# The first image of a convolution and attention block: one set of filter sums in another buffer, another order of the first loads, and BatchNorm's factors on GpSimd

## The chip, the core and the metric

The kernel runs on one core of a Trainium2 chip. Such a core has TensorE (PE: matrix products), VectorE (DVE), ScalarE (ACT), GpSimd (POOL) and SyncE (SP, which here issues transfers), each with an instruction stream of its own; they wait for each other through semaphores. On-chip memory is SBUF; products land in PSUM. The metric is the device time of one execution in microseconds (us). The kernel before takes 2331.0 us, the median of three runs (2330.74 to 2331.12).

## The reference

The input is a batch of eight images of 512 channels and 32x32 positions. All is float32. `silu`, `softmax` and 3x3 convolutions are the usual ones; `bn` is BatchNorm with given mean and variance.

```python
# x: (8, 512, 32, 32); C = 256, N = 2 blocks, 4 heads of 64
def cbs(x, w, p, pad):
    return silu(bn_eval(conv2d(x, w, pad), p))

def bot_attention(x, qkv_w, rw, rh):
    qkv = conv2d(x, qkv_w, 0)                       # 1x1
    q, k, v = ...                                   # (8, 4, 64, 1024) each
    logits = einsum('bhdi,bhdj->bhij', q, k + rw + rh) * 64 ** -0.5
    return einsum('bhij,bhdj->bhdi', softmax(logits), v)

def block(x):
    t = cbs(x, cv1_w, cv1_bn, 0)                    # 1x1, 512 -> 512
    ys = [t[:, :C], t[:, C:]]                       # y0, y1
    for i in range(N):
        z = cbs(ys[-1], m_cv1_w[i], m_cv1_bn[i], 1)     # 3x3, 256 -> 256
        z = bot_attention(z, m_qkv_w[i], m_rw[i], m_rh[i])
        z = silu(bn_eval(conv2d(z, m_cv2_w[i], 0), m_cv2_bn[i]))
        ys.append(ys[-1] + z)
    return cbs(concatenate(ys, axis=1), cv2_w, cv2_bn, 0)

out = x + block(group_norm(x, 32 groups))
```

## The kernel before

The kernel goes through the images one after the other. TensorE's stages of an image are: `cv1` (a 1x1 convolution; in the program `ps`, line 386), the first 3x3 convolution (`c_ps`, line 970), the projections to q, k, v, the attention (`l_ps`, `av_ps`), `m2` (`m_ps`, line 994), the second 3x3 convolution, its attention, and the last 1x1 convolution. The `cv1` of the next image is done in pieces inside the attention of the image before it. VectorE, ScalarE and GpSimd prepare operands and read results.

**Filter sums.** The 3x3 convolutions work on sums of taps and sums of pixels, so that fewer products are needed. The sums of pixels, `v_in`, come from `tiles_in`; the sums of taps, `u`, come from the raw taps by `make_u`. There are three kinds (pairs 0, 1, 2), two halves of output channels (`oc`) and two halves of input channels (`k`). They are made once, during the first image, stored to DRAM and loaded for the later ones.

```python
def make_u(i, u, raw):
    rows, g1 = raw
    g0, g2 = rows[:, 0], rows[:, 1]
    ...
    if i == 2:
        nc.scalar.copy(u[:, :, 0:3:2], rows[:, :, 0::2])
        tt(minus, ...); tt(plus, ...); return tt(minus, ...)     # lines 331 to 333
    if i == 0:
        tt(b, g0, g2, ALU.add); tt(a, ...); tt(b, ...)           # lines 335 to 337
    else:
        stt(b, g2, 4.0, g0, ...); stt(a, ...); stt(b, ...)       # lines 339 to 341
    tt(minus, ...); tt(plus, ...); return stt(minus, ...)        # lines 343 to 345
```

**The ring.** Large weights and filter sums share five buffers under one name; a new tile waits until one of the five is read for the last time.

```python
def ring(shape, name):
    return const.tile(shape, F32, tag="u", name=name, bufs=5)

def new_u(name):
    return ring([P, NM, 2, NC, P], name)

def make(n, oc, pairs, ks=range(NM)):
    for k in ks:
        for i in pairs:
            if k == 0:
                us[oc, i] = new_u("u_new")
            last = make_u(i, us[oc, i][:, k], raws[n, oc, k])
            if k == NM - 1:
                nc.gpsimd.dma_start(u_dram[n][oc][i], us[oc, i])
    return last
```

**The first loads.** Transfers are issued in this order; a chunk of `x` is 512 KB, a piece of raw taps 576 KB, each half of `w1` 512 KB (two of its four row blocks).

```python
xs = [load_x(act, 0, c, NX) for c in range(NX // 2)]       # chunks 0 and 1
...
raws = {(0, 0, 0): load_raw(0, 0, 0, "k")}
load_w1_half(0)
xs += [load_x(act, 0, c, NX) for c in range(NX // 2, NX)]  # chunks 2 and 3
...
load_w1_half(1)
raws[0, 0, 1] = load_raw(0, 0, 1, "v")
... # BatchNorm's parameters, the other raws, the weights of the blocks
```

**The start.** GroupNorm is done in two parts, chunks 0 and 1, then 2 and 3. `tc.issue_after(x)` only tells the scheduler that what follows stands behind `x`.

```python
_, _, (_, read, _) = s.group_norm_part(xs[: NX // 2])
norm = s.group_norm_part(xs[NX // 2 :])
with tc.issue_after(read.ins):
    with tc.issue_after(loaded.ins):
        made = make_u(2, u_first[2][:, 0], raws[0, 0, 0])
    next(norm)
...
with tc.issue_after(made.ins):                              # BatchNorm's factors
    nc.vector.tensor_scalar(rstd, bnp[:, :, 3], BN_EPS, None, ALU.add)
    nc.gpsimd.tensor_tensor(rstd, rstd, mhalf[:, :NBN], ALU.pow)
    made = make_u(0, u_first[0][:, 1], raws[0, 0, 1])
with tc.issue_after(made.ins):
    nc.vector.tensor_tensor(sh, bnp[:, :, 0], rstd, ALU.mult)
    nc.vector.tensor_tensor(bh, bnp[:, :, 2], sh, ALU.mult)
    nc.vector.tensor_tensor(bh, bnp[:, :, 1], bh, ALU.subtract)
    for at in bn_m1:
        last = nc.vector.tensor_scalar(sh[:, at : at + NM], ..., -1 / 12, None, ALU.mult)
```

**From the first attention to the second convolution.** `behind` holds work that is put between pieces of the attention. In image 0 this is how the filter sums of block 1 come about: `u(1, 0, ..)` first, then of the second half pair 2 (which is only stored and loaded again later), pair 0, and after the attention pair 1.

```python
ao, check = s.attention_fast(0, z, b * N * NM * NH, behind, sq.get(0), t)
made = make(1, 1, [1]) if b == 0 else None
with tc.issue_after(made.ins) if made else nullcontext():
    last = s.m2(0, ao, y1, lambda oc, half: inner(y2, oc, half))    # adds at line 1002
if six: ...
elif more:
    s.cv1(w1, xs, nxt, y1n, Y0S)         # image 0: the last two pieces of the next cv1
vs = s.tiles_in(y2)
z, t = s.conv3x3(1, vs, u_of(1), True)
```

At the end of the attention `second()` loads the raw taps for pair 1 where k and v of the attention were: `raws[1, 1, k] = load_raw(1, 1, k, "kv"[k])`. The tile `q` is written by the projections, read by the logits and written again by the projections of the next block.

Of the kernel before, what the change touches and what calls it, by code (L numbers as in the profile page):

```python
# [44 lines left out]
F32 = mybir.dt.float32  # L45
I32 = mybir.dt.int32
AF = mybir.ActivationFunctionType
ALU = mybir.AluOpType
# [4 lines left out]
P = 128  # L53
BN_EPS = 1e-3
# [7 lines left out]
def kernel(  # L62
# [16 lines left out]
    nc = tc.nc  # L79
# [4 lines left out]
    NX = C1 // P  # L84
    NM = C // P
# [8 lines left out]
    NC = 4  # L94
# [3 lines left out]
    act = fast.enter_context(tc.tile_pool(name="act", bufs=1))  # L98


    def load_x(pool, b, c, bufs):
        xt = pool.tile([P, HW], F32, tag="x", name="x", bufs=bufs)
        src = x[b, ts(c, P), :] if isinstance(b, int) else x[bass.ds(b, 1), ts(c, P), :][0]
        nc.sync.dma_start(xt, src)
        return xt

    xs = [load_x(act, 0, c, NX) for c in range(NX // 2)]


    def ring(shape, name):  # L110
        return const.tile(shape, F32, tag="u", name=name, bufs=5)
# [8 lines left out]
    def load_w1_half(i):  # L120
        ks = slice(i * NX // 2, (i + 1) * NX // 2)
        nc.sync.dma_start(w1[:, ks], cv1_w.rearrange("(k p) o -> p k o", p=P)[:, ks])
# [9 lines left out]
    def rows_of_raw(raw):  # L132
        rows = raw.rearrange("p (r c) o -> p r c o", c=3)
        return rows[:, 0::2], rows[:, 1]

    def load_raw(n, oc, k, tag, bufs=1):
        raw = act.tile([P, 9, P], F32, tag=tag, name="raw", bufs=bufs)
        nc.sync.dma_start(raw, m_cv1_w[n, ts(k, P), :, ts(oc, P)])
        return rows_of_raw(raw)
# [11 lines left out]
        return rows_of_raw(raw[:, 0:9]), (both, mid)  # L151

    raws = {(0, 0, 0): load_raw(0, 0, 0, "k")}
    load_w1_half(0)
    xs += [load_x(act, 0, c, NX) for c in range(NX // 2, NX)]

# [40 lines left out]
    bnp = const.tile([P, NBN, 4], F32, name="bnp")  # L197
# [117 lines left out]
    def new_u(name):  # L315
        return ring([P, NM, 2, NC, P], name)
# [9 lines left out]
        stt, tt = nc.vector.scalar_tensor_tensor, nc.vector.tensor_tensor  # L326
        a, b = u[:, 0, 0:3], u[:, 1, 0:3]
        plus, minus = u[:, :, 1], u[:, :, 3]
        if i == 2:
            nc.scalar.copy(u[:, :, 0:3:2], rows[:, :, 0::2])  # L330
            tt(minus, rows[:, :, 0], rows[:, :, 2], ALU.add)
            tt(plus, minus, rows[:, :, 1], ALU.add)
            return tt(minus, minus, rows[:, :, 1], ALU.subtract)
        if i == 0:
            tt(b, g0, g2, ALU.add)
            tt(a, b, g1, ALU.add)
            tt(b, b, g1, ALU.subtract)
        else:
            stt(b, g2, 4.0, g0, ALU.mult, ALU.add)
            stt(a, g1, 2.0, b, ALU.mult, ALU.add)  # L340
            stt(b, g1, -2.0, b, ALU.mult, ALU.add)

        tt(minus, u[:, :, 0], u[:, :, 2], ALU.add)
        tt(plus, minus, plus, ALU.add)
        return stt(minus, minus, 2.0, plus, ALU.mult, ALU.subtract)

    def load_u(n, oc, i):
        u = new_u("u")
        nc.sync.dma_start(u, u_dram[n][oc][i])
        return u  # L350
# [10 lines left out]
    def inner(yp, c, half):  # L361
        return yp[:, c, 1 + half * ROWS : 1 + (half + 1) * ROWS, :].rearrange("p h w -> p (h w)")

    def stages(act, small, ps_big, ps_av, n_pt):
# [120 lines left out]
        def gn_stats(mv, c, xt):  # L485
            st = small.tile([P, NH, 6], F32, tag="st", name="st")
            for half in range(NH):
                nc.vector.bn_stats(st[:, half, :], xt[:, ts(half, HALF)])
            nc.vector.bn_aggr(mv[:, c, :], st.rearrange("p a b -> p (a b)"))
# [9 lines left out]
        def gn_mean(mv, n=NX, pool=ps_big, tag="big"):  # L499

            ps = pool.tile([P, n], F32, tag=tag, name="gm_ps")
            over_groups(ps, mv[:, :, 0])
            gm = small.tile([P, n], F32, tag="gm", name="gm")
            dev = small.tile([P, n], F32, tag="dev", name="dev")
            nc.vector.tensor_copy(gm, ps)
            nc.vector.tensor_tensor(dev, mv[:, :, 0], gm, ALU.subtract)
            nc.vector.tensor_tensor(dev, dev, dev, ALU.mult)
            averaged = nc.vector.tensor_tensor(dev, dev, mv[:, :, 1], ALU.add)
            return gm, dev, averaged
# [9 lines left out]
        def group_norm_part(xts):  # L519


            n = len(xts)
            mv = small.tile([P, n, 2], F32, tag="mv", name="mv", bufs=2)
            for c in range(n):
                gn_stats(mv, c, xts[c])
            yield
            gm, dev, averaged = gn_mean(mv, n, ps_av, "av")
            yield averaged
            gr, multiplied, read = gn_rstd(dev, n, ps_av, "av")
            shift = small.tile([P, n], F32, tag="dev", name="shift")  # L530
            nc.gpsimd.tensor_tensor(shift, gm, gr, ALU.mult)
            nc.gpsimd.tensor_scalar(shift, shift, -1.0, None, ALU.mult)
            for c in range(n):
                for half in range(NH):
                    part = xts[c][:, ts(half, HALF)]
                    applied = nc.scalar.activation(
                        part, part, AF.Identity, scale=gr[:, c : c + 1], bias=shift[:, c : c + 1]
                    )
            yield multiplied, read, applied

        def group_norm(xts):

# [708 lines left out]
    s = stages(act, small, ps_big, ps_av, 3)  # L1251
# [4 lines left out]
    Y0S, Y1S = range(NM), range(NM, 2 * NM)  # L1256
    us = {}

    def make(n, oc, pairs, ks=range(NM)):

        for k in ks:
            for i in pairs:
                if k == 0:
                    us[oc, i] = new_u("u_new")
                last = make_u(i, us[oc, i][:, k], raws[n, oc, k])
                if k == NM - 1:
                    nc.gpsimd.dma_start(u_dram[n][oc][i], us[oc, i])
        return last

    loaded = s.table_of(AF.Silu)  # L1270
    u_first = [new_u("u_new") for _ in range(PAIRS)]
# [1 line left out]
        us[0, i] = u_first[i]  # L1273

    Y_ORDER = [*Y1S, *Y0S]
    _, _, (_, read, _) = s.group_norm_part(xs[: NX // 2])
    norm = s.group_norm_part(xs[NX // 2 :])
    with tc.issue_after(read.ins):
        with tc.issue_after(loaded.ins):
            made = make_u(2, u_first[2][:, 0], raws[0, 0, 0])  # L1280
        next(norm)
    with tc.issue_after(made.ins):
        made = make_u(0, u_first[0][:, 0], raws[0, 0, 0])
    begun = {}

    def begin(oc, ks):
        begun[oc] = s.cv1_products(w1, xs, oc, ks, begun.get(oc))
        return s.last_product[0]
# [4 lines left out]
    with tc.issue_after(averaged.ins):  # L1293
        made = make_u(1, u_first[1][:, 0], raws[0, 0, 0])
    begin(Y_ORDER[0], [1])
    first = begin(Y_ORDER[1], [0])
    with tc.issue_after(first.ins):
        multiplied, normed, applied = next(norm)
    with tc.issue_after(multiplied.ins):
        begin(Y_ORDER[1], [1])  # L1300
        begin(Y_ORDER[2], range(NX // 2))
    with tc.issue_after(made.ins):
        nc.vector.tensor_scalar(rstd, bnp[:, :, 3], BN_EPS, None, ALU.add)
        nc.gpsimd.tensor_tensor(rstd, rstd, mhalf[:, :NBN], ALU.pow)
        made = make_u(0, u_first[0][:, 1], raws[0, 0, 1])
    with tc.issue_after(made.ins):
        nc.vector.tensor_tensor(sh, bnp[:, :, 0], rstd, ALU.mult)
        nc.vector.tensor_tensor(bh, bnp[:, :, 2], sh, ALU.mult)
        nc.vector.tensor_tensor(bh, bnp[:, :, 1], bh, ALU.subtract)

        for at in bn_m1:
            last = nc.vector.tensor_scalar(sh[:, at : at + NM], sh[:, at : at + NM], -1 / 12, None, ALU.mult)
    with tc.issue_after(last.ins), tc.issue_after(applied.ins):
        for i in (1, 2):
            made = make_u(i, u_first[i][:, 1], raws[0, 0, 1])
    for i in range(PAIRS):
        nc.gpsimd.dma_start(u_dram[0][0][i], u_first[i])
    last = made
# [6 lines left out]
    for b in range(B):  # L1325
# [36 lines left out]
        norm = s.group_norm(xs) if more else iter(())  # L1362
# [50 lines left out]
        else:  # L1413
            behind[-1] = lambda: make(1, 0, range(PAIRS))
        ao, check = s.attention_fast(0, z, b * N * NM * NH, behind, sq.get(0), t)
        made = make(1, 1, [1]) if b == 0 else None
        with tc.issue_after(made.ins) if made else nullcontext():
            last = s.m2(0, ao, y1, lambda oc, half: inner(y2, oc, half))
        if six:
# [62 lines left out]
        last = s.m2(1, ao, y2, lambda oc, half: ylast[:, oc, ts(half, HALF)])  # L1482
# [27 lines left out]
    with tc.If(held < P):  # L1510
        with ExitStack() as gs:
# [7 lines left out]
            with tc.For_i(0, B, 1) as b:  # L1519
# [6 lines left out]
                for n in range(N):  # L1526
                    z, _ = g.conv3x3(n, g.tiles_in(yi), lambda oc: [load_u(n, oc, i) for i in range(PAIRS)])
# [58 lines left out]
```

## Time and profile before

| | |
|---|---|
| time, median of 3 | 2331.0 us |
| span of the profiled run | 2329.5 us |
| TensorE busy | 2289.5 us (98%) |
| VectorE busy | 1839.0 us (79%) |
| ScalarE busy | 988.3 us (42%) |
| GpSimd busy | 89.1 us (4%) |
| moved by DMA | 235.60 MB, mean 101 GB/s |
| mean granted TensorE clock | 0.995 |

The profile names groups of instructions by line of the program, engine, operation, and tiles "out<-in". In a timeline a row has start, duration, engine, line, operation, tiles, shape, count and, in brackets, how long the engine was idle before it and what it waited for. The view of waits has total, number and longest wait in us. The view of stretches gives for each stretch the busy time of PE, PEld (loading of weights), DVE, ACT and POOL with their counts, then the granted TensorE clock, the DMA's busy share and GB/s. In the page's table of slices each digit is the busy share of one fortieth of the span in tenths. A wait for several semaphores is put down to the one that came last, so the name of the releaser has to be checked against what it can have released. Every float32 product stands in the trace as two records, and a few records are missing.

### The profile page before, as it was taken

The numbers are of one execution on the slowest core, as the hardware profiler recorded it, in microseconds if no ns is written. First come the engines' busy times: TensorE is split into PE (matmuls) and PEld (weight loads), VectorE is DVE, ScalarE is ACT, GpSimd is POOL, SyncE is SP. The second block draws the span as 40 slices with busy tenths as digits, with TensorE's granted clock in tenths as the row PEclk, the third lists the DMA queues.
The fourth block names the chain that finished last, engine by engine and source line by source line (L and its number), as shares of the span: only waits on it lengthen the run. The fifth ranks groups of instructions, "written<-read, shape, count | busy, mean of one in ns | idle before, by whom it ended". The sixth has DMA issues, their size and how long they took to land.

```text
span 2329.5 us, 36531 instructions
## 1 busy us (share of the span) xinstructions
PE 2289.5 (98%) x14806; PEld 1174.3 (50%) x14806; DVE 1839.0 (79%) x2920; ACT 988.3 (42%) x1292; POOL 89.1 (4%) x308
## 2 busy tenths in 40 slices
PE   7997999999999999999999999999999999999998
PEld 4545346363464635546364463645536364473643
DVE  8867877879778887888878877888877888777774
ACT  2442523536245362444525445253543535435352
POOL 1000000000000000000000000000000000000000
PEclk9998999999999999999999999999999999999999
DMA  7422226031250414304152131612216031260201
GB/s 237 173 67 104 78 96 230 16 133 48 95 193 15 150 34 141 145 15 150 33 195 95 46 114 51 236 40 78 84 47 248 29 117 43 60 235 16 86 11 61
DMA packets 95521, 235.60 MB, mean 101 GB/s; under 512 B 28016, under 2 KB 50736, under 8 KB 81904
## 3 DMA queue, kind: packets, MB, share of 16 engines
q1 hardware_dynamic: 83600, 182.84, 23.1%
q0 software_dynamic: 11744, 50.34, 5.6%
q8 instruction: 119, 1.95, 0.3%
q14 instruction: 58, 0.48, 0.1%
HBM read 198.54 MB, written 34.60 MB: 100 GB/s over the span
## 4 chain that ended last, share of the span: by engine, by line
PE 95%; DVE 4%; ACT 0%; DMA 0%; POOL 0%; issue 0%; DVEq 0%; ACTq 0%
PE av_ps L768 19%; PE l_ps L734 19%; PE c_ps L970 14%; PE c L1028 8%; PE p_ps L630 8%; PE x_ps L1140 6%; PE c_new L1028 6%; PE m_ps L994 5%; PE ps L386 4%; PE pv_ps L634 3%; PE s_ps L786 1%; PE p_ps L634 1%; PE s_ps L804 1%; DVE acc L754 0%; DVE v_in L445 0%; PE v_ps L595 0%
## 5 line engine op out<-in xcount | busy, mean ns | idle before, releaser
L738 ACT ACTIVATE pt<-l_ps 128x1024 f32<-128x1024 f32 x512 | 495.0, 1023 | 410.0 <-PE l_ps L734 385.2
L754 DVE TENSOR_TENSOR acc<-acc,pt 128x1024 f32<-128x1024 f32 x384 | 469.6, 1223 | 65.4 <-ACT pt L738 40.4
L768 PE MATMUL av_ps<-pt,vT 64*64 64x512 f32 x4096 | 486.4, 591 | 0.5 <-DVE ao L776 0.5
L734 PE MATMUL l_ps<-q,kr 64*64 64x512 f32 x4096 | 485.9, 590 | 0.0
L970 PEld LDWEIGHTS c_ps<-v_in,u 128*128 128x128 f32 x2720 | 306.0, 192 | 6.7 <-issue 6.7
L970 PE MATMUL c_ps<-v_in,u 128*128 128x128 f32 x2720 | 306.1, 275 | 0.0
L768 PEld LDWEIGHTS av_ps<-pt,vT 64*64 64x64 f32 x4096 | 159.1, 133 | 269.4 <-issue 225.7
L734 PEld LDWEIGHTS l_ps<-q,kr 64*64 64x64 f32 x4096 | 160.0, 133 | 263.3 <-issue 252.2
L452 ACT COPY m<-c_ps 128x256 f32<-128x256 f32 x96 | 35.5, 370 | 230.0 <-PE c_ps L970 227.3
L1028 PE MATMUL c_new<-t_in,ws 128*128 128x512 f32 x288 | 124.6, 592 | 0.0
L994 PE MATMUL m_ps<-ao,m_sb 128*128 128x512 f32 x256 | 112.5, 592 | 0.0
L369 ACT ACTIVATE m_kept<-m_kept,bh,sh 128x512 f32<-128x512 f32 x42 | 32.0, 809 | 145.9 <-DVE m_kept L1112 86.3
L752 DVE TENSOR_TENSOR acc<-pt 128x1024 f32<-128x1024 f32 x64 | 78.1, 1221 | 18.0 <-ACT pt L738 18.0
L1028 PEld LDWEIGHTS c_new<-t_in,ws 128*128 128x128 f32 x288 | 54.7, 190 | 68.9 <-issue 66.0
L630 PE MATMUL p_ps<-t_z,sq 128*128 128x512 f32 x180 | 87.1, 593 | 0.0
L369 ACT ACTIVATE t<-m_ps,bh,sh 128x512 f32<-128x512 f32 x64 | 48.1, 777 | 87.9 <-PE m_ps L994 82.4
L994 PEld LDWEIGHTS m_ps<-ao,m_sb 128*128 128x128 f32 x256 | 48.6, 190 | 61.2 <-issue 61.2
L1002 DVE TENSOR_TENSOR ylast<-t,ypad 128x512 f32<-128x512 f32 x32 | 22.0, 693 | 63.2 <-ACT t L369 63.2
L369 ACT ACTIVATE z<-z,bh,sh 128x512 f32<-128x512 f32 x64 | 48.7, 809 | 53.2 <-DVE z L481 53.2
L445 DVE TENSOR_TENSOR v_in<-w_rows 128x512 f32<-128x512 f32 x96 | 66.3, 691 | 0.0
L1028 PE MATMUL c<-ypad,ws 128*128 128x512 f32 x144 | 63.8, 592 | 0.0
L453 DVE TENSOR_TENSOR r_mid<-c_ps,m 128x256 f32<-128x256 f32 x64 | 27.2, 426 | 45.8 <-ACT m L452 45.8
(255 smaller groups left out, 3009.0 us busy)
## 6 DMA issues: line engine op xcount, KB each, us to landing
u<-u SPq DMA_DIRECT2D x85, 1024.0 KB
x<-in_x_dram SPq DMA_DIRECT2D x32, 512.0 KB
x_res<-in_x_dram POOLq DMA_DIRECT2D x32, 512.0 KB, 6.9
out_dram<-m_kept POOLq DMA_DIRECT2D x28, 512.0 KB, 7.4
u<-u_new POOLq DMA_DIRECT2D x12, 1024.0 KB, 6.8
w<-in_cv_w_dram SPq DMA_DIRECT2D x12, 1024.0 KB
rs<-r_dram SPq DMA_DIRECT2D x96, 128.0 KB
ws<-s SPq DMA_DIRECT2D x24, 512.0 KB
```

What stands on the lines that cost most here:

```text
L369: return nc.scalar.activation(dst, src, AF.Silu, scale=sh[:, k : k + 1], bias=bh[:, k : k + 1])
L386: last_product[0] = nc.tensor.matmul(ps[:, half, :], w_of(k), rhs_of(k, half), start=(k == begin), stop=(k == end))
L630: nc.tensor.matmul(ps[:, o, :], w[:, o, :], rhs, start=not onto, stop=True, skip_group_check=onto)
L634: nc.tensor.matmul(v[:, ts(j, P)], rhs[:, ts(j, P)], w[:, 2, :], start=j == 0 and not onto, stop=True, skip_group_check=True,)
L734: nc.tensor.matmul(ps[kh * HD : (kh + 1) * HD, hd, :], kr[r, c, o : o + HD], q[r, c, ts(half, HALF)], start=True, stop=True,)
L738: exp = nc.scalar.activation(pt[:, i], ps, AF.Exp, scale=SCALE)
L754: ins = nc.vector.tensor_tensor(accs[g], accs[g], pt[:, i], ALU.add)
L768: nc.tensor.matmul(avs[g][hd * HD : (hd + 1) * HD, kh, :], vT[r, j, o : o + HD], pt[r, i, hd, :], start=(j == 0), stop=(j == NJ - 1),)
L970: nc.tensor.matmul(ps[:, row, col, :], us[i][:, k, row, SLOT[col], :], vs[i][:, k, row, col, :], start=(k == 0), stop=(k == NM - 1),)
L994: nc.tensor.matmul(pss[oc][:, half, :], m2_sb[:, n, k, ts(oc, P)], ao[:, k, ts(half, HALF)], start=(k == 0), stop=(k == NM - 1),)
L1028: nc.tensor.matmul(ps[:, o, :], w[:, k, ts(o, P)], rhs[part][:, c, :], start=(k == 0 and not onto), stop=(k == KB - 1), skip_group_check=onto,
L1140: nc.tensor.matmul(ps[:, o, :], w[:, c, ts(o, P)], rhs[c], start=(c == 0 and not onto), stop=(c == 1), skip_group_check=onto,)
```

## The change

Three things are changed, all in the first image.

1. The filter sums of block 1, second half, pair 1 are written into the place of `q` instead of a ring buffer. It is meant to free them of the wait for a ring buffer.
2. The raw taps of the first filters are loaded between chunk 0 and chunk 1 of `x`, and their sums of pair 2 are no longer held behind GroupNorm's first part. It is meant to give VectorE work while it waits for `x`.
3. The factors of BatchNorm (`rstd`, `sh`, `bh`) are made by GpSimd alone, behind GroupNorm's second part. It is meant to take work off VectorE in a stage in which it is busy.

```diff
-    xs = [load_x(act, 0, c, NX) for c in range(NX // 2)]
+    xs = [load_x(act, 0, 0, NX)]
 ...
     raws = {(0, 0, 0): load_raw(0, 0, 0, "k")}
+    xs.append(load_x(act, 0, 1, NX))
     load_w1_half(0)
 ...
-    def make(n, oc, pairs, ks=range(NM)):
+    def make(n, oc, pairs, ks=range(NM), place=None):
 ...
-                    us[oc, i] = new_u("u_new")
+                    us[oc, i] = place or new_u("u_new")
 ...
+    with tc.issue_after(loaded.ins):
+        made = make_u(2, u_first[2][:, 0], raws[0, 0, 0])
     with tc.issue_after(read.ins):
-        with tc.issue_after(loaded.ins):
-            made = make_u(2, u_first[2][:, 0], raws[0, 0, 0])
         next(norm)
 ...
+    with tc.issue_after(shifted.ins):
+        nc.gpsimd.tensor_scalar(rstd, bnp[:, :, 3], BN_EPS, None, ALU.add)
+        nc.gpsimd.tensor_tensor(rstd, rstd, mhalf[:, :NBN], ALU.pow)
+        nc.gpsimd.tensor_tensor(sh, bnp[:, :, 0], rstd, ALU.mult)
+        nc.gpsimd.tensor_tensor(bh, bnp[:, :, 2], sh, ALU.mult)
+        nc.gpsimd.tensor_tensor(bh, bnp[:, :, 1], bh, ALU.subtract)
+
+        for at in bn_m1:
+            nc.gpsimd.tensor_scalar(sh[:, at : at + NM], sh[:, at : at + NM], -1 / 12, None, ALU.mult)
     with tc.issue_after(made.ins):
-        nc.vector.tensor_scalar(rstd, bnp[:, :, 3], BN_EPS, None, ALU.add)
-        nc.gpsimd.tensor_tensor(rstd, rstd, mhalf[:, :NBN], ALU.pow)
         made = make_u(0, u_first[0][:, 1], raws[0, 0, 1])
-    with tc.issue_after(made.ins):
-        nc.vector.tensor_tensor(sh, bnp[:, :, 0], rstd, ALU.mult)
-        nc.vector.tensor_tensor(bh, bnp[:, :, 2], sh, ALU.mult)
-        nc.vector.tensor_tensor(bh, bnp[:, :, 1], bh, ALU.subtract)
-
-        for at in bn_m1:
-            last = nc.vector.tensor_scalar(sh[:, at : at + NM], sh[:, at : at + NM], -1 / 12, None, ALU.mult)
-    with tc.issue_after(last.ins), tc.issue_after(applied.ins):
+    with tc.issue_after(made.ins), tc.issue_after(applied.ins):
         for i in (1, 2):
             made = make_u(i, u_first[i][:, 1], raws[0, 0, 1])
 ...
-        made = make(1, 1, [1]) if b == 0 else None
+        made = None
+        if b == 0:
+            made = make(1, 1, [1], place=act.tile([P, NM, 2, NC, P], F32, tag="q", name="u_new"))
```

`shifted` is the last GpSimd instruction of GroupNorm's second part. In the built program the twelve `make_u` instructions of (1) stand, on VectorE, ahead of the last reciprocal of the first attention; before they stood behind it. The order of TensorE's instructions is the same in both.

More of the change, by code (lines that the diff above doesn't have):

```diff
@@ L531, in group_norm_part @@
             nc.gpsimd.tensor_tensor(shift, gm, gr, ALU.mult)
-            nc.gpsimd.tensor_scalar(shift, shift, -1.0, None, ALU.mult)
+            shifted = nc.gpsimd.tensor_scalar(shift, shift, -1.0, None, ALU.mult)
             for c in range(n):
@@ L538, in group_norm_part @@
                     )
-            yield multiplied, read, applied
+            yield multiplied, read, applied, shifted
         def group_norm(xts):
@@ L1275 @@
     Y_ORDER = [*Y1S, *Y0S]
-    _, _, (_, read, _) = s.group_norm_part(xs[: NX // 2])
+    _, _, (_, read, _, _) = s.group_norm_part(xs[: NX // 2])
     norm = s.group_norm_part(xs[NX // 2 :])
+    with tc.issue_after(loaded.ins):
+        made = make_u(2, u_first[2][:, 0], raws[0, 0, 0])
     with tc.issue_after(read.ins):
-        with tc.issue_after(loaded.ins):
-            made = make_u(2, u_first[2][:, 0], raws[0, 0, 0])
         next(norm)
@@ L1297 @@
     with tc.issue_after(first.ins):
-        multiplied, normed, applied = next(norm)
+        multiplied, _, applied, shifted = next(norm)
     with tc.issue_after(multiplied.ins):
```

## The prediction, made before the result was known

> **What bounds the kernel now.** I read the page first, then TensorE's chain of waits, then the timeline around the longest wait, then the clock by stretches.
>
> ```profile
> PE 2289.5 (98%) x14806; PEld 1174.3 (50%) x14806; DVE 1839.0 (79%) x2920; ACT 988.3 (42%) x1292; POOL 89.1 (4%) x308
> PE   7997999999999999999999999999999999999998
> ```
>
> TensorE is busy for 98% of 2329.5 us. Only 40 us of the span are idle, and the fourth slice (175 to 233 us) is one of two that show it. So no change to the first image can win more than about that. The waits of TensorE over the whole span say where:
>
> ```profile
> PE c_ps L970 <- DVE v_in L445: 13.6, 3, 11.4
> PE gm_ps L496 <- DVE mv L489: 7.5, 1, 7.5
> PE c_ps L970 <- DVE u_new L344: 3.2, 1, 3.2
> PE ps L386 <- ACT x L536: 2.7, 1, 2.7
> PE ps L386 <- ACT y L369: 1.5, 1, 1.5
> ```
>
> All lie before 210 us, in image 0. The largest, 11.4 us, is the start of the second 3x3 convolution. The timeline there:
>
> ```profile
> 179.15 7.13 PE L386 MATMUL ps<-x,w 128*128 128x512 f32 x16 [1.54 <-ACT y L369]
> ...
> 186.32 1.03 DVE L339 SCALAR_TENSOR_TENSOR u_new<-raw 128x384 f32<-128x384 f32 x2 [23.24 <-DMA w_half<-in_cv_w_dram]
> ...
> 191.14 1.29 DVE L1002 TENSOR_TENSOR ypad<-t,ypad 128x512 f32<-128x512 f32 x2
> 191.53 0.54 POOL L1267 DMA_DIRECT2D u<-u_new  x1 [34.39 <-DVE u_new L345]
> 191.87 1.45 ACT L369 ACTIVATE t<-m_ps,bh,sh 128x512 f32<-128x512 f32 x2 [4.10 <-DVE ypad L1002]
> ```
>
> The vector engine does nothing for 23.24 us and starts `u_new` 0.04 us after TensorE's last `ps` product (179.15 + 7.13 = 186.28). The DMA that the row names writes another tile; what came free at 186.28 is the ring buffer of `w1`, which that product read last. Four ring buffers hold `u(0,0..2)` and `u(1,0)` of block 1, the fifth `w1`; so `make(1, 1, [1])` waits for `w1`. The adds of `m2` are ordered behind it, the input tiles `v_in` behind the adds, the convolution behind those. Then the clock:
>
> ```profile
> 186.00:198.00 12.00, 0.61 (x2) 0.35 (x2) 11.44 (x26) 2.90 (x4) 0.71 (x3) 0.66 0.22 89
> ...
> 200.00:202.00 2.00, 2.00 (x10) 2.00 (x11) 2.00 (x6) 0.00 (x0) 0.00 (x0) 0.50 0.03 8
> ...
> 204.00:206.00 2.00, 2.00 (x21) 2.00 (x20) 2.00 (x5) 0.37 (x1) 0.17 (x2) 1.00 0.00 0
> ```
>
> After the gap TensorE works at half its clock (0.50) until about 203.4 us: 10 matmul records in 2 us instead of 21. The end and the full pace of the convolution:
>
> ```profile
> 220.39 3.74 PE L970 MATMUL c_ps<-v_in,u 128*128 128x128 f32 x32
> 223.96 1.88 PE L630 MATMUL p_ps<-z,qkv_sb 128*128 128x512 f32 x4
> ```
>
> A sixth of the convolution (32 records) takes 223.96 - 220.39 = 3.57 us undisturbed, all of it 21.4; in the second image it takes 21.27.
>
> For the first stage, the timeline of the start and then that of the first convolution:
>
> ```profile
> 11.65 1.29 DVE L488 BATCH_NORM_STATS2 st<-x 128x6 f32<-128x512 f32 x2 [1.00 <-DMA x<-in_x_dram]
> 11.92 4.71 PE L386 MATMUL ps<-x,w 128*128 128x512 f32 x6 [2.72 <-ACT x L536]
> ...
> 22.63 3.17 POOL L1304 TENSOR_TENSOR rstd<-rstd,mhalf 128x16 f32<-128x16 f32 x1 [0.55 <-DVE rstd L1303]
> ```
>
> ```profile
> 42.17 11.55 PE L970 MATMUL c_ps<-v_in,u_new 128*128 128x128 f32 x102
> 56.89 11.90 PE L970 MATMUL c_ps<-v_in,u_new 128*128 128x128 f32 x90 [3.17 <-DVE u_new L344]
> ```
>
> TensorE starts at 11.92, runs without a listed wait to 53.7 and stops for the sums of the second half of the filters. The vector engine has no idle time there from 25.83 to 65.5: it is the bound of this stage.
>
> **What the Trainium skill says.** "TensorE: Matmul & The Clock Gate" (Part 1: The HAM clock gate): an idle window of some 3.4 us halves the clock, a busy one restores it, and the windows run freely. The trace agrees: 0.50 after the 11.4 us gap, and 0.74 on the average from 58 to 62 us after the gap of 3.17. "SBUF — State Buffer" (Who interferes with whom): a vector instruction with two SBUF inputs and a GpSimd instruction that reads SBUF lock each other out. The trace shows no harm to the vector engine: beside the 3.17 us power by GpSimd (22.63) its two-input ops keep their 0.55 us. "GPSIMD Engine Reference" (4.1 Engine selection): two-input work is about twice as slow there. The trace: 0.31 to 0.46 us on 128x2 against 0.16 on the vector engine.
>
> **Part 1: the sums leave the ring.** `q` is last read by the logits (about 145 us), `kr` and `vT` by 148.7, so the raw taps can come. Four transfers (two raws, two stores of `sq`) keep the DMA above 0.9 from 152 to 158. In the built order the twelve instructions now stand before the last reciprocal. Six form a chain of 3.1 us (0.55 + 0.58 + 0.59 + 3 x 0.45 with the gaps between, as at 17.92 to 22.47). Sums of k = 0 about 155.0 to 158.1; eviction of `ao` (0.68) to 158.8; sums of k = 1 to 161.9; add 0.6, reciprocal 3.35, scale 0.7: 166.6 instead of 163.1. Only the sixth of eight `m2` products needs that: 163.71 + 5 x 0.88 = 168.1. Hidden, with 1.5 us to spare.
>
> The four SiLUs of `m2` then follow at 169.1, 170.8, 171.6, 172.4 and the adds end near 174.4. The tiles of pairs 0, 1, 2 take about 5 us each and are done near 179.5, 184.6 and 189.2. Needed at 184.7, 188.3 and 191.8: never late. As both tiles of `m2` in PSUM are free by 173.2, I take it that `ps` no longer waits for the SiLU of the one before it (1.54 us).
>
> Sum: from the end of the third `ps` (177.61) to the end of the convolution, before 223.96 - 177.61 = 46.35 us; after 7.03 + 21.4 = 28.43. **Gain 17.9** (waits 11.39 + 1.35 + 0.86 + 1.54 = 15.1, cold clock 2.8). Behind it TensorE is busy without a listed wait, so the gain stays. The reload of `u(1,2)` takes the buffer of `w1`: about 4 us in a stage where it has 14.
>
> **Part 2: raws between the chunks.** The second chunk of `x` comes after 576 KB more. The DMA moved its first 1.05 MB by about 5.3 us and 0.58 MB more by 7.6; so its statistics begin near 7.6 instead of 5.89, and TensorE near 13.6 instead of 11.92. The third and fourth chunk come as before. In return three sums (1.4 us) fill the wait. But the means of the second half stand on TensorE behind three products at the cold clock, which begin later: the vector engine idles about 2.3 us before `gm` at 19.0. Nearly nothing is won there.
>
> **Part 3: BatchNorm's factors.** The vector engine loses seven instructions, 1.0 us, and a wait of 0.25. GpSimd starts at about 24 and needs 0.4 + 3.2 + 3 x 0.5 + 2 x 0.45, so until 30.0; the first SiLU then has its product at 30.3 (before 28.64 + 1.7). It just fits.
>
> Parts 2 and 3 together bring the vector engine to `L340` of the second raw about 0.8 us sooner (25.7 for 26.50). From there to 76 us it hardly idled, so it bounds this stage. In the new order `u(1,0)` is complete at 52 instead of 57.8, and TensorE's wait of 3.17 us goes, but the next sums (pairs 1 and 2) end only at about 63.4 against 64.5, and their products wait for those. The input `z` of the projections is there some 0.4 us sooner. **Gain 0.3**, as the wait is moved, not removed.
>
> Sum: 2331.0 - 17.9 - 0.3 = 2312.8 us. I add 0.4 for the risks below: **2313.2**.
>
> **Rivals.** (a) The 1.54 us wait stays, if the fourth `ps` is still given the PSUM buffer of the third: 2314.3. For: both orders show it waiting for ScalarE; against: the other two buffers are free 4 us sooner. (b) The clock: if the split wait at 58 to 63 us makes a cold window, 44 records run partly at half pace and `z` comes 0.5 to 1.5 us late instead of early: 2313.5 to 2314.5. For: a gap of 3.17 did it before; against: some matmuls fall into it. (c) The vector engine takes over the bound at 155 to 168: if the raws land 2 us later than I read, `m2` waits and the adds slip, but the tiles keep 5 us of slack: under 1 us. (d) GpSimd's chain is slowed by the lock and holds up the first SiLU by 1 to 2 us; that lands on the busy vector engine: 2314 to 2315. (e) The second chunk's delay is not absorbed and all of its 1.7 us goes to the end: 2314.5. None gives back 17.9 us.
>
> **Range and chances.** Part 1 is read from measured pieces and could miss by 1.5; parts 2 and 3 are a small difference of large sums, -1.5 to +2.5. So 2310.5 to 2316.5 in eight of ten cases. Two per cent would be 46.6 us, more than all idle time: faster by over 2% 0.005; slower by over 2% needs a new wait of 65 us, 0.01; within 2% 0.985.
>
> **What would show it.** Part 1: no wait for `v_in` near 186 us, the clock at 1.00 from 180 to 210, `u_new` inside 154 to 163, the second convolution begun near 185 and ended near 206. The wait for `y` absent, or 1.5 us: rival a. Part 2: TensorE's first product near 13.6. Part 3: POOL busy 24 to 30, first `ypad` near 30.3. The first convolution's end within 1 us of 68.8, with waits for `u_new` or a lower clock between 58 and 66. I am wrong if `u_new` still waits for a buffer, or if a wait appears behind 230 us where there was none.

## The result, and the profile after

| | before | after |
|---|---|---|
| time, median | 2331.06 us (4 runs) | 2318.62 us (4 runs, 2317.30 to 2319.48) |
| ratio, 95% interval | | 0.9946 [0.9928, 0.9963] |
| span of the profiled run | 2329.5 us | 2317.9 us |
| mean granted TensorE clock | 0.995 | 0.997 |

The change wins 12.4 us. The prediction was 2313.2 us, with 2310.5 to 2316.5 as its range: the result lies 5.4 us above the number and 2.1 us outside the range. Line numbers have moved by one to three; `L971` of after is `L970` of before.

The page of after, its busy times and the slices of TensorE:

```profile
PE 2288.9 (99%) x14806; PEld 1174.6 (51%) x14806; DVE 1838.3 (79%) x2914; ACT 987.4 (43%) x1292; POOL 94.8 (4%) x314
PE   7999999999999999999999999999999999999998
```

The fourth slice is full now; the first still shows idle time, and the last, as it did before. The same work is done in a span that is 11.6 us shorter. TensorE's waits over the whole span of after (total, number, longest, in us):

```profile
PE gm_ps L497 <- DVE mv L490: 11.0, 1, 11.0
PE ps L387 <- ACT x L537: 2.7, 1, 2.7
PE c_ps L971 <- DVE u_new L341: 2.4, 1, 2.4
...
PE c_ps L971 <- DVE u_new L345: 0.8, 1, 0.8
PE c_ps L971 <- DVE r_ends L457: 0.7, 1, 0.7
```

The 13.6 us for `v_in` and the 1.5 us for `y` are gone. In their place the first wait, for the statistics of `x`, has grown from 7.5 to 11.0, and three waits inside the first convolution (0.7, 2.4 and 0.8) stand where one of 3.2 stood.

The timeline of TensorE in after, at the second convolution, and its clock in the stretches that the prediction looked at:

```profile
177.35 13.90 PE L387 MATMUL ps<-x,w 128*128 128x512 f32 x32
191.09 18.03 PE L971 MATMUL c_ps<-v_in,u_new 128*128 128x128 f32 x160
208.95 3.74 PE L971 MATMUL c_ps<-v_in,u 128*128 128x128 f32 x32
212.52 1.88 PE L631 MATMUL p_ps<-z,qkv_sb 128*128 128x512 f32 x4
```

```profile
186.00:198.00 12.00, 12.00 (x75) 9.13 (x74) 11.96 (x31) 1.82 (x3) 0.52 (x6) 1.00 0.70 230
200.00:202.00 2.00, 2.00 (x20) 2.00 (x19) 1.68 (x5) 0.00 (x0) 0.00 (x0) 1.00 0.92 342
204.00:206.00 2.00, 2.00 (x20) 2.00 (x20) 1.35 (x3) 0.52 (x1) 0.00 (x0) 1.00 1.02 382
```

No bracket, so no wait, and 20 records in 2 us at clock 1.00 where there were 10 at 0.50. The third `ps` ends in the middle of the 32 records, at 177.35 + 6.95 = 184.30; from there to the end of the convolution it is 28.2 us, before 46.35. This part of the change brought what it was meant to bring. But before, this group ended at 223.96, and now at 212.52: only 11.4 us earlier, because the stage starts late. The first stage of after, first VectorE's start, then TensorE to the projections:

```profile
8.07 0.42 DVE L332 TENSOR_TENSOR u_new<-raw 128x256 f32<-128x256 f32 x1 [2.16 <-DMA raw<-in_m_cv_w_dram]
8.53 0.42 DVE L333 TENSOR_TENSOR u_new<-u_new,raw 128x256 f32<-128x256 f32 x1
8.98 0.42 DVE L334 TENSOR_TENSOR u_new<-u_new,raw 128x256 f32<-128x256 f32 x1
9.37 1.28 DVE L489 BATCH_NORM_STATS2 st<-x 128x6 f32<-128x512 f32 x2
```

```profile
15.47 5.49 PE L387 MATMUL ps<-x,w 128*128 128x512 f32 x6 [2.74 <-ACT x L537]
...
46.52 14.68 PE L971 MATMUL c_ps<-v_in,u_new 128*128 128x128 f32 x130
61.89 0.68 PE L971 MATMUL c_ps<-v_in,u_new 128*128 128x128 f32 x4 [0.69 <-DVE r_ends L457]
65.01 1.38 PE L971 MATMUL c_ps<-v_in,u_new 128*128 128x128 f32 x6 [2.44 <-DVE u_new L341]
67.16 8.45 PE L971 MATMUL c_ps<-v_in,u_new 128*128 128x128 f32 x52 [0.77 <-DVE u_new L345]
75.44 3.60 PE L387 MATMUL ps<-z,qkv_sb 128*128 128x512 f32 x8
```

The statistics of the second chunk begin at 9.37 (before 5.89), TensorE at 15.47 (before 11.92), the projections at 75.44 (before 68.63). From then on everything is late by 6.8 us. The GpSimd rows of after, where BatchNorm's factors are made, and the first SiLU:

```profile
27.04 3.04 POOL L1305 TENSOR_TENSOR rstd<-rstd,mhalf 128x16 f32<-128x16 f32 x1
30.16 4.57 POOL L1306 TENSOR_TENSOR sh<-bnp,rstd 128x16 f32<-128x16 f32 x1
34.80 0.22 POOL L1307 TENSOR_TENSOR bh<-bnp,sh 128x16 f32<-128x16 f32 x1
```

```profile
35.35 2.78 ACT L370 ACTIVATE ypad<-ps,bh,sh 128x512 f32<-128x512 f32 x4 [5.57 <-POOL bh L1308]
36.83 0.69 DVE L423 SCALAR_TENSOR_TENSOR w_tmp<-ypad 128x512 f32<-128x512 f32 x1 [2.19 <-ACT ypad L370]
```

One multiplication of 16 columns takes 4.57 us, the next, of the same size, 0.22. The first SiLU comes at 35.35 (before 28.64) and VectorE stands still for 2.19 us.

### The profile page after: what moved, and what is told of

It is laid out like the page before. It is cut to its first block, busy times and chain, and to the rows that moved or that the text cites. A ratio compares the mean times of both kernels' runs of the same rounds, so it can differ in the third digit from the quotient of the medians.

```text
span 2317.9 us, 36534 instructions
## 1 busy us (share of the span) xinstructions
PE 2288.9 (99%) x14806; PEld 1174.6 (51%) x14806; DVE 1838.3 (79%) x2914; ACT 987.4 (43%) x1292; POOL 94.8 (4%) x314
## 4 chain that ended last, share of the span: by engine, by line
PE 96%; DVE 3%; POOL 0%; ACT 0%; DMA 0%; issue 0%; SPq 0%; DVEq 0%; POOLq 0%; ACTq 0%
PE av_ps L769 19%; PE l_ps L735 19%; PE c_ps L971 14%; PE c L1029 8%; PE p_ps L631 8%; PE x_ps L1141 6%; PE c_new L1029 6%; PE m_ps L995 5%; PE ps L387 4%; PE pv_ps L635 3%; PE s_ps L787 1%; PE p_ps L635 1%; PE s_ps L805 1%; DVE acc L755 0%; DMA raw<-in_m_cv_w_dram 0%; PE v_ps L596 0%
## 5 line engine op out<-in xcount | busy, mean ns | idle before, releaser
L971 PEld LDWEIGHTS c_ps<-v_in,u 128*128 128x128 f32 x2720 | 306.0, 192 | 6.7 <-issue 6.7
L971 PE MATMUL c_ps<-v_in,u 128*128 128x128 f32 x2720 | 306.2, 275 | 0.0
```

Of the source, the lines that this page charges most:

```text
L971: nc.tensor.matmul(ps[:, row, col, :], us[i][:, k, row, SLOT[col], :], vs[i][:, k, row, col, :], start=(k == 0), stop=(k == NM - 1),)
```

## The experiments

Two causes were in question. **A**: the factors come late, because GpSimd is locked out. **B**: the second chunk of `x` comes late, because the raw taps stand before it. A third theory formed on the way, **C**: neither delay counts as such, only the time in which VectorE stands still before 45 us. From 45 to 60 us it is busy without a gap in every kernel here.

All runs in one table. "Idle" is 45 us less VectorE's busy time in that stretch, "z" the start of the projections (`ps<-z`), both of the profiled run, whose own time is given beside them. The experiments ran in three groups (e1 to e4, e5 to e8, e9 to e12), each on another chip. The kernel before took 2331.9, 2332.5 and 2331.3 us in them and 2331.1 beside after, and e5_after_again lies 0.7 us below after where before lies 1.4 above; so a difference between groups can be off by 1 to 2 us.

| run | median us | profiled | TensorE's start | idle | z |
|---|---|---|---|---|---|
| before | 2331.06 | 2331.06 | 11.92 | 9.11 | 68.63 |
| after | 2318.62 | 2319.34 | 15.47 | 13.78 | 75.44 |
| e1_place_only | 2313.13 | 2313.22 | 12.25 | 9.62 | 69.55 |
| e2_place_loads | 2318.15 | 2318.30 | 14.58 | 12.40 | 74.76 |
| e3_place_factors | 2312.43 | 2311.72 | 12.05 | 9.02 | 67.66 |
| e4_sums_behind | 2317.01 | 2314.73 | 15.66 | 11.60 | 70.50 |
| e5_after_again | 2317.96 | 2318.23 | 15.75 | 13.21 | 74.39 |
| e6_sums_only | 2315.60 | 2314.68 | 13.71 | 10.61 | 70.12 |
| e7_sums_wait | 2317.75 | 2317.72 | 15.14 | 12.83 | 73.60 |
| e8_early_factors | 2312.96 | 2312.67 | 12.17 | 9.50 | 68.35 |
| e9_x1_later | 2318.90 | 2318.42 | 17.46 | 14.29 | 73.98 |
| e10_fill_idle | 2312.44 | 2312.10 | 14.98 | 10.41 | 68.06 |
| e11_gr_later | 2313.38 | 2313.22 | 12.01 | 9.36 | 68.14 |
| e12_sums_first | 2310.22 | 2310.30 | 12.02 | 8.72 | 66.25 |

Profiled time less z is 2262.4 in before and 2243.5 to 2245.1 in all thirteen others, mean 2244.1. So the place of `q` brings 17.4 to 18.9 us in them, 18.3 on the average, and nearly all else that tells these kernels apart has happened by the start of the projections.

**The change in pieces.** Part 1 alone:

```diff
-        made = make(1, 1, [1]) if b == 0 else None
+        made = None
+        if b == 0:
+            made = make(1, 1, [1], place=act.tile([P, NM, 2, NC, P], F32, tag="q", name="u_new"))
```

> Only the first part of the change: the sums of pair 1 go to the place of q; loads and BatchNorm's factors stay as in the kernel before. Both theories (A: the late factors of BatchNorm cost the first stage its time; B: the late second chunk of x does) put the whole loss into the first stage, so both expect the full gain of the first part, 18 us: 2313 us (2312 to 2314), TensorE's first product at 11.9, no wait for v_in near 186, and the second convolution ended 28 us after the third ps. If the time is above 2315, part of the 18 us is given back later and both theories are too small.

Measured 2313.13 (2312.99 to 2313.57), as both expected: 18.7 less than before in the same group. Parts 1 and 2, with BatchNorm's factors made as before:

```diff
-    with tc.issue_after(shifted.ins):
-        nc.gpsimd.tensor_scalar(rstd, ...)          # and the rest of the factors
+    with tc.issue_after(made.ins):
+        nc.vector.tensor_scalar(rstd, bnp[:, :, 3], BN_EPS, None, ALU.add)
+        ...                                         # as in the kernel before
```

> Parts 1 and 2: sums in the place of q, raw taps between the chunks of x; BatchNorm's factors again on VectorE and GpSimd as in the kernel before. A (the factors): the first SiLU comes by 31 to 32 us instead of 35.4, and the time is near 2313. B (the loads): TensorE starts at 15.5, as in the changed kernel, and most of the loss stays: 2316 to 2318. If both causes lie in series on VectorE, 2315 to 2317.

Measured 2318.15 (2316.49 to 2319.06). The first SiLU came at 32.32, close to the 31 to 32 that A had, but the time stayed: part 2 alone costs 5.0 us on top of part 1. A falls as the main cause. Parts 1 and 3, with the loads of before:

```diff
-    xs = [load_x(act, 0, 0, NX)]
+    xs = [load_x(act, 0, c, NX) for c in range(NX // 2)]
 ...
-    xs.append(load_x(act, 0, 1, NX))
```

and the sums of pair 2 behind `read` again.

> Parts 1 and 3: sums in the place of q, BatchNorm's factors by GpSimd behind GroupNorm's second part; loads as in the kernel before. A: GpSimd's multiply for sh again takes over 3 us and ends only when VectorE's two-input instructions pause; the first SiLU comes near 33 instead of 28.6 and the time is 2315 to 2318. B: the factors do no harm without the late start: TensorE begins at 11.9 and the time is 2313 to 2314.

Measured 2312.43 (2311.72 to 2312.79): part 3 alone wins 0.7 us, and here GpSimd's multiplication took 0.25 us and the first SiLU came at 28.93. Then the changed kernel with only the sums put back:

```diff
-    with tc.issue_after(loaded.ins):
-        made = make_u(2, u_first[2][:, 0], raws[0, 0, 0])
     with tc.issue_after(read.ins):
+        with tc.issue_after(loaded.ins):
+            made = make_u(2, u_first[2][:, 0], raws[0, 0, 0])
         next(norm)
```

> The changed kernel, but the sums of pair 2 are again held behind the statistics of chunks 0 and 1; the raw taps are still loaded between the chunks. The three sums (1.3 us) no longer stand ahead of the second chunk's statistics, so TensorE begins near 14.2 instead of 15.5. B: the time falls by as much, to 2317.3. A: the sums are then in the way later, the first SiLU stays at 35 or comes later, and the time stays at 2318 to 2319.

TensorE's start did not move (15.66). The timeline of VectorE in this run says why:

```profile
5.71 0.21 DVE L490 BATCH_NORM_AGGREGATE mv<-st 128x2 f32<-128x12 f32 x1
9.40 0.69 DVE L489 BATCH_NORM_STATS2 st<-x 128x6 f32<-128x512 f32 x1 [3.49 <-DMA x<-in_x_dram]
```

With no sums in front of it VectorE waits for the chunk itself until 9.40. So it is the transfer that is late. The three sums of after, which end at 9.40, filled a wait and delayed little or nothing; how much is not known, as the landing varies (in e2_place_loads VectorE waited for it until 8.49). The time, 2317.01 (2314.73 to 2317.57), is near what B expected, but not for B's reason, an earlier start.

The next run separates the order of the sums from the order of the loads:

> Part 1 and only the second half of part 2: loads in the order of before, but the sums of pair 2 no longer held behind GroupNorm's first part; on VectorE the three sums then stand between the statistics of chunk 1 and the copy gm. The raw taps land near 7.5 to 8, so gm moves from 8 to 9.3 or 9.7, TensorE begins near 13.5 instead of 12.0. If VectorE is the bound of the stage, only its idle time counts, which hardly changes: 2313 to 2314. If the start of TensorE counts, 2314.5 to 2315.5.

This run (part 1, loads of before, sums of pair 2 free) took 2315.60 (2314.68 to 2316.55). On VectorE the sums stand ahead of `gm` and wait for the raw taps until 8.70; TensorE starts at 13.71. Against e1_place_only the idle time rises by 1.0 us, the time by 2.5, in the profiled run by 1.5. The times speak for the late start. The start of the projections does not: it rises by only 0.57 us (69.55 to 70.12), less than the idle time; the other 0.9 us of the profiled difference lie behind it, where the two kernels have the same work. As the two runs are of different groups, this one does not decide.

**Is the start the cost, or the idle time?** First the second chunk still later:

```diff
-    xs.append(load_x(act, 0, 1, NX))
     load_w1_half(0)
+    xs.append(load_x(act, 0, 1, NX))
```

> The changed kernel with the second chunk of x loaded still later, behind the first half of w1 (512 KB more, about 1.3 us at the 390 GB/s that the trace shows there). If the landing of the second chunk drives the loss, TensorE's first product comes near 17 instead of 15.5 to 15.75 and the time rises by 1 to 2 us, to 2319 to 2320.5. If the start does not matter, 2318.

TensorE's start moved to 17.46, 1.7 to 2.0 us later than in after; the time is 2318.90 (2318.42 to 2319.93), 0.3 to 0.9 more than the two groups of after (2318.62, 2317.96), just below what was expected if the start counts, and within what two groups can differ by. Idle time rose by 0.5 to 1.1 only, and the projections began at 73.98, sooner than in after (75.44) and e5_after_again (74.39), although TensorE had started later. That speaks against the start as the cost. Then the start left late and the idle time filled:

```diff
-    with tc.issue_after(averaged.ins):
-        made = make_u(1, u_first[1][:, 0], raws[0, 0, 0])
+    made = make_u(1, u_first[1][:, 0], raws[0, 0, 0])
```

> The changed kernel with one tie taken away: the sums of pair 1 need not stand behind the means of GroupNorm's second part, so VectorE has them to do in the 2.2 to 3.1 us in which it waits for gm; TensorE still starts at 15.5. If VectorE's idle time is the cost, the time falls by 2.5 to 4 us, to 2314 to 2315.5, and TensorE's waits near 60 to 67 shrink. If the late start of TensorE is the cost, it stays near 2318.

Measured 2312.44 (2312.10 to 2312.83): one scheduling tie away, and the change is 5.5 to 6.2 us faster, with TensorE still starting at 14.98, 3 us later than in before. That is more than was expected of C (2314 to 2315.5). The wait of VectorE for `gm`, in after and then in this run:

```profile
21.24 0.16 DVE L506 COPY gm<-gm_ps 128x2 f32<-128x2 f32 x1 [3.08 <-PE gm_ps L497]
```

```profile
19.88 0.16 DVE L506 COPY gm<-gm_ps 128x2 f32<-128x2 f32 x1 [0.45 <-PE gm_ps L497]
...
34.39 0.69 DVE L423 SCALAR_TENSOR_TENSOR w_tmp<-ypad 128x512 f32<-128x512 f32 x1 [1.59 <-ACT ypad L370]
```

The gap at `gm` shrank from 3.08 to 0.45, the one behind the late factors from 2.19 to 1.59. TensorE in this run:

```profile
45.16 15.12 PE L971 MATMUL c_ps<-v_in,u_new 128*128 128x128 f32 x134
61.14 7.08 PE L971 MATMUL c_ps<-v_in,u_new 128*128 128x128 f32 x58 [0.85 <-DVE u_new L345]
68.06 3.60 PE L387 MATMUL ps<-z,qkv_sb 128*128 128x512 f32 x8
```

It starts the convolution 1.4 us sooner than after and ends it 7.4 us sooner; 3.4 us of this are less idle time (13.78 - 10.41). Part of the rest the edit brings of itself, because it changes the order of the sums: e12_sums_first below has the same edit on e3_place_factors. With part 3 in all four, the medians are

| | sums of pair 1 tied | free |
|---|---|---|
| loads and sums of before | 2312.43 (e3) | 2310.22 (e12) |
| part 2 | 2318.62, 2317.96 (after, e5) | 2312.44 (e10) |

So part 2 costs 5.5 to 6.2 us where VectorE has nothing to do at `gm`, and 2.2 us where it has. So 3.3 to 4.0 us of its cost are no cost of a late start: in both cases TensorE starts some 3 us later. The 2.2 us that stay go with 10.41 - 8.72 = 1.7 us more idle time of VectorE.

The table allows a closer check, because in z the noise of what follows is left out. If C holds, z less the idle time depends on VectorE's work and its order alone, and not on TensorE's start:

| kernels with the same work | TensorE's start | z less idle |
|---|---|---|
| factors as before: before, e1, e6 | 11.92, 12.25, 13.71 | 59.5, 59.9, 59.5 |
| factors by GpSimd: e3, e8, e11, e4 | 12.05, 12.17, 12.01, 15.66 | 58.6, 58.9, 58.8, 58.9 |
| the same, sums of pair 1 free: e12, e10 | 12.02, 14.98 | 57.5, 57.7 |

A start that comes 1.5 to 3.6 us later moves z by no more than 0.3 us beyond the idle time. The five others (after, e2, e5, e7, e9) lie at 59.7 to 62.4, above the rows to which they belong by their work; what they have in common comes next.

**The second effect, the clock.** The idle time of after exceeds that of e3_place_factors, which has the same VectorE work, by 13.78 - 9.02 = 4.8 us, but z comes 7.8 later. The stretches of after from 60 us on (busy time of PE, PEld, DVE, ACT and POOL; the last three columns are granted clock, DMA share, GB/s):

```profile
60.00:66.00 6.00, 2.87 (x21) 2.52 (x20) 6.00 (x17) 1.89 (x3) 0.00 (x0) 0.95 0.40 123
66.00:70.00 4.00, 3.23 (x15) 2.94 (x15) 4.00 (x13) 0.00 (x0) 1.06 (x2) 0.50 0.23 98
66.00:76.00 10.00, 9.23 (x56) 8.70 (x56) 7.62 (x23) 0.69 (x2) 1.06 (x2) 0.69 0.67 251
```

and the same of e4_sums_behind:

```profile
60.00:66.00 6.00, 3.33 (x24) 2.76 (x24) 6.00 (x18) 1.89 (x3) 0.53 (x1) 1.00 0.51 164
66.00:70.00 4.00, 4.00 (x38) 4.00 (x38) 3.86 (x12) 0.37 (x1) 0.53 (x1) 1.00 0.90 371
66.00:76.00 10.00, 9.18 (x55) 6.81 (x55) 9.86 (x28) 1.82 (x4) 0.53 (x1) 1.00 0.89 311
```

TensorE is idle for 3.1 and 2.7 us from 60 to 66 us. In after the clock then falls to 0.50, and the last 52 records take 8.45 us; in e4_sums_behind it holds, and 54 records take 6.63 (64.03 to 70.66). That is 8.45 - 52/54 x 6.63 = 2.1 us. VectorE idles then, for it waits for those products:

```profile
73.42 0.42 DVE L454 TENSOR_TENSOR r_mid<-c_ps,m 128x256 f32<-128x256 f32 x1 [2.38 <-ACT m L453]
```

4.8 + 2.1 = 6.9 of the 7.8 us. The remaining 0.9 us lie in the order of VectorE's instructions, which is another in after. TensorE's last wait for a sum ends at 67.16 there, and in e3_place_factors at 61.52:

```profile
61.52 6.29 PE L970 MATMUL c_ps<-v_in,u_new 128*128 128x128 f32 x54 [1.32 <-DVE u_new L344]
```

Less the idle time these are 67.16 - 13.78 = 53.4 and 61.52 - 9.02 = 52.5 us of VectorE's work: in after it comes to that sum 0.9 us of work later. The clock's share is read from the traces; no edit separates it. That e4's profiled run took 2314.73 and its other three 2316.9 to 2317.6 at a lower mean clock (0.997 to 0.998 against 0.999) fits the clock going either way at the same waits, though those three have no trace here.

**The lock.** The changed kernel once more, unaltered:

> The changed kernel once more, unaltered: 2317 to 2319.5 us. It asks whether GpSimd's multiply for sh (4.57 us in the first profile) is always so long. If VectorE's gapless two-input instructions lock it out by rule, it takes over 3 us again and ends with VectorE's pause near 34.6. If it is chance, it can be near 0.3 to 0.5 us, as in the kernels with parts 1 and 3 (0.25) and with the sums held behind (0.46), and the first SiLU comes near 31.5.

Measured 2317.96 (2317.69 to 2318.38). Again 4.57 us, so it was no chance of one run:

```profile
26.45 3.03 POOL L1305 TENSOR_TENSOR rstd<-rstd,mhalf 128x16 f32<-128x16 f32 x1
29.56 4.57 POOL L1306 TENSOR_TENSOR sh<-bnp,rstd 128x16 f32<-128x16 f32 x1
34.21 0.22 POOL L1307 TENSOR_TENSOR bh<-bnp,sh 128x16 f32<-128x16 f32 x1
```

Then VectorE held still while GpSimd works:

```diff
+    with tc.issue_after(made.ins):
+        made = nc.vector.tensor_copy(rstd[:, 0:1], bh[:, 0:1])
     with tc.issue_after(made.ins), tc.issue_after(applied.ins):
         for i in (1, 2):
```

> The changed kernel with a small copy of bh on VectorE ahead of its last sums of the first half, so that VectorE stands still while GpSimd makes sh and bh. If the two-input instructions lock GpSimd out: sh takes 0.2 to 0.3 us instead of 4.57, bh is there at 31, the first SiLU at 31.2 instead of 35.35; VectorE idles 2.8 us instead of 2.2, so the time is 2317.5 to 2319.5. If sh is slow of itself, it still takes over 3 us and the time rises by 3 us or more.

```profile
25.48 3.03 POOL L1305 TENSOR_TENSOR rstd<-rstd,mhalf 128x16 f32<-128x16 f32 x1
28.59 0.23 POOL L1306 TENSOR_TENSOR sh<-bnp,rstd 128x16 f32<-128x16 f32 x1
28.90 0.22 POOL L1307 TENSOR_TENSOR bh<-bnp,sh 128x16 f32<-128x16 f32 x1
```

0.23 for 4.57: GpSimd was locked out by VectorE. What VectorE was doing in after at that time:

```profile
33.42 0.41 DVE L344 TENSOR_TENSOR u_new<-u_new 128x256 f32<-128x256 f32 x1
33.75 0.55 DVE L337 TENSOR_TENSOR u_new<-u_new,raw 128x384 f32<-128x384 f32 x1
34.22 0.42 DVE L345 TENSOR_TENSOR u_new<-u_new 128x256 f32<-128x256 f32 x1
36.83 0.69 DVE L423 SCALAR_TENSOR_TENSOR w_tmp<-ypad 128x512 f32<-128x512 f32 x1 [2.19 <-ACT ypad L370]
```

Sums of two pairs are interleaved, so each starts before the one ahead of it has ended (33.42 + 0.41 > 33.75): there is no gap. The last ends at 34.64, GpSimd's multiplication at 34.73. "SBUF — State Buffer" (Who interferes with whom) of the Trainium skill says that a VectorE instruction with two SBUF inputs and a GpSimd instruction that reads SBUF exclude each other; the runs agree, and show that it can go against GpSimd for eleven instructions in a row. It need not: in e3_place_factors and e4_sums_behind, beside the same interleaved sums, the multiplication took 0.25 and 0.46 us. What the lock costs was not separated: e7_sums_wait pays for its freedom with 2.81 us of idle VectorE and is as slow as after (2317.75), and e10_fill_idle is the faster one with a multiplication of 3.54 us.

**Two attempts at less idle time in e3_place_factors.**

```diff
     with tc.issue_after(first.ins):
-        multiplied, _, applied, shifted = next(norm)
+    with tc.issue_after(first.ins), tc.issue_after(made.ins):
+        multiplied, _, applied, shifted = next(norm)
```

> Parts 1 and 3 with the loads of before (2312.43), and VectorE's read gr of the second part put behind the sums of pair 1, so that VectorE does not wait 1.7 us for TensorE ahead of them. If VectorE's idle time is the cost, 1.7 us less: 2310.5 to 2311.5. GroupNorm's second part comes 0.9 us later; if TensorE or the first SiLU waits for it, 2312 to 2313.

Measured 2313.38 (2313.22 to 2313.63), above both ranges and nearer to the second. The 1.7 us of waiting for `gr` did go, but the later multiplication took 2.06 us beside the sums, the first SiLU came at 29.61 instead of 28.93 and VectorE waited 2.20 for it: idle 9.36 for 9.02. The wait was moved. The other puts the edit of e10_fill_idle into e3_place_factors:

> Parts 1 and 3 with the loads of before, and the sums of pair 1 no longer tied behind the means of GroupNorm's second part, as in the run that fills the idle time. VectorE then has sums to do in its waits for gm and gr (0.6 and 1.7 us): 2310.5 to 2312. If the order of the sums that results makes the convolution wait elsewhere, 2313 or more.

Measured 2310.22 (2309.71 to 2310.36), the fastest here: 8.4 us less than the change, with the least idle time (8.72) and one wait of 0.86 in the first convolution. It contains parts 1 and 3, not part 2. Last, the factors moved ahead of GroupNorm's second part:

> Parts 1 and 3 with the loads of before, but GpSimd makes BatchNorm's factors behind GroupNorm's first part, where it idles from 11.0 to 20.3, not behind the second. The parameters land near 14, the power ends near 18, sh and bh before 20. If the late factors held anything up in the kernel with parts 1 and 3 (2312.43), this is faster, 2311 to 2312; if VectorE's work alone is the bound there, 2312.2 to 2312.8. If the power runs into GroupNorm's second part: 2313 or more.

Inconclusive: the tie only says what the factors stand behind, and in the built program GpSimd's order is that of e3_place_factors (the factors begin at 22.99, behind the second part). The run repeats that kernel: 2312.96 for 2312.43, in another group.

## Why the prediction was right and wrong

**Part 1, right.** Gain 17.9 predicted; 18.3 by the table, 18.7 by e1_place_only. No wait for `v_in`, clock 1.00, 28.2 us for 28.43. (The 21.27 us given for a later convolution is a row that lacks 3 of 192 records; whole ones there take 21.4, as the estimate had it.) The twelve instructions ran from 162.3 to 169.1, and the `ao` product that waits for the reciprocal ended at 173.8; less the 6.8 us by which the stage is late, that is 155.5 to 162.3 and 167.0, for 155.0 to 161.9 and 166.6 predicted. The wait of 1.54 did vanish (rival a falls).

**Part 2, the step that failed.** "So its statistics begin near 7.6 instead of 5.89, and TensorE near 13.6": measured 8.49 to 9.64 and 14.6 to 15.8 in the runs with this order of loads. The estimate took the chunk as there when as many bytes had been moved as were issued up to it. In e4_sums_behind VectorE could begin on it when the DMA had moved 2.4 MB, in e2_place_loads 2.1 MB, by the stretches of 1 us; the chunk and all that was issued ahead of it are 1.64 MB. So the engines had moved 0.5 to 0.8 MB of the transfers behind it by then. For the first chunk the same reading gives 0.1 to 0.2 MB, so the time between landing and start is not the whole of it. The pace varied as well: 1.64 MB were moved by 7.3 to 8.1 us.

"The vector engine idles about 2.3 us before `gm`": 2.2 and 3.1 in the two profiles of after, so about right. "Nearly nothing is won there" then left this out of the sum, although the next paragraph says that VectorE "bounds this stage". That is the error that counts: the sum had VectorE sooner by 0.8 us, at `L340` of the second raw at 25.7, and in after it came there at 28.12:

```profile
28.12 0.55 DVE L340 SCALAR_TENSOR_TENSOR u_new<-raw 128x384 f32<-128x384 f32 x1
```

In e3_place_factors, without part 2, it came there at 25.66. Together with the 2.2 us behind the late factors these are the 4.8 us of idle time that make up the larger part of the 7.8. e2_place_loads puts part 2 at 5.0 us lost.

**Part 3, half right.** Alone it wins 0.7, near the 0.8 us that VectorE was to gain. "It just fits" (GpSimd done at 30.0, first SiLU 30.3) held in e3_place_factors, 28.93, and also in e4_sums_behind with the late loads, 32.05, where the SiLU waits for TensorE. It failed in after, where sh and bh were ready at 35.3: the term of 0.5 us for each multiplication was 4.57 for one.

**The sum.** "Parts 2 and 3 together: gain 0.3" is a loss of 5.5 (2318.62 - 2313.13). The rivals were named and too small: (e), the delay not absorbed, 1.7 us, in fact 5.0 with all that follows; (b), the cold clock, 0.5 to 1.5, in fact 2.1; (d), the lock, 1 to 2, in fact 4.1 us on GpSimd and 2.2 of VectorE's idle time. They came together, where the range had taken them one at a time. The sign of rival (e) was right, its reason was not: TensorE's late start is absorbed to within 0.3 us, and VectorE's idle time is not.

## What to carry to other kernels

Where one engine is gapless up to the end of a stage, count a change by that engine's idle time before it, not by when another engine starts: with ready work in a gap of 3 us, the same late transfer cost 2.2 us and not 5.5. A transfer put ahead of one that a chain waits for can delay it by more than its own bytes: here 2.6 to 3.5 us where 1.7 had been counted. Waits that are split into several short ones can still cost the clock (2.1 us here). Small GpSimd work beside interleaved two-input VectorE work may not get done until VectorE pauses (4.57 us here for 0.23), so put it where VectorE is quiet.

## What the runs showed of the hardware that was not expected

- The lock can starve GpSimd: 4.57 us in two runs, 4.34, 3.54, 3.54 and 2.06 in others, for a multiplication of 0.23. In e10_fill_idle it ended at 31.97, when the sums of one pair alone were left, each waiting for the one before it: those start 0.45 us apart and last 0.41 to 0.43. Yet in e3_place_factors and e4_sums_behind it took 0.25 and 0.46, and VectorE's instructions there grew by some 0.03 us each for a moment. What lets GpSimd in at the one time and not at the other stays open.
- A transfer issued third can be ready for use only when 0.5 to 0.8 MB of those behind it have been moved too. "DMA: Bandwidth & Descriptors" (Two DMAs through the same engine are not ordered) of the Trainium skill says that descriptors start in order but are pipelined and need not finish so; the landings here fit that, though no run separates it from other delays between the last byte and the start on it.
- TensorE idle for 2.1 to 3.7 of the 6 us from 60 to 66 went with a clock below 0.9 from 66 to 76 us in five profiles (after, e2, e5, e7, e9), and 2.7 us idle did not in another (e4). "TensorE: Matmul & The Clock Gate" (Part 1: The HAM clock gate) of the Trainium skill has the windows run freely; that would explain the difference, which no run here tests.
